# One more query product by Strassen's scheme in 128 columns, and a new order of work in a step, in a fused attention kernel

## The chip, the cores and the metric

The kernel runs on one core of a Trainium2 chip. The core has five engines with instruction queues of their own, each worked off in order: TensorE (PE: matmuls into PSUM, with weight loads beside them), VectorE (DVE), ScalarE (ACT), GpSimd (POOL) and SyncE (SP, which here issues nearly all DMAs). They meet through semaphores: an instruction waits until the ones it needs are done, and all behind it on its queue wait with it. The metric is the device time of one execution in microseconds (us), the median of several runs.

## The reference

All is float32: 64 batches of 128 tokens with 512 features, 16 heads of 64, one key and one value head for all of them.

```python
def layernorm(x, g):
    mean = jnp.mean(x, axis=-1, keepdims=True)
    var = jnp.var(x, axis=-1, keepdims=True)
    return (x - mean) * jax.lax.rsqrt(var + EPS) * g

xn = layernorm(x, g_in)
q = (xn @ Wq).reshape(b, n, H, DH).transpose(0, 2, 1, 3) * scale
kv = xn @ Wkv
k, v = (kv[..., :DH], kv[..., DH:])
# a null key and value are put ahead of k and v
sim = jnp.einsum('bhid,bjd->bhij', q, k)
sim = sim + bias
# causal mask, then the mask of the batch
attn = jax.nn.softmax(sim, axis=-1)
out = jnp.einsum('bhij,bjd->bhid', attn, v)
out = out.transpose(0, 2, 1, 3).reshape(b, n, INNER)
out = out @ Wo
result = x + layernorm(out, g_out)
```

## The kernel before

The 64 batches go in 32 steps of two. Step `d` treats batches `a = 2d` and `b = 2d + 1`: their scores and softmax. In the same step it does the attention over the values and the output projection for the pair before (`p`, `p + 1`, with `p = 2d - 2`), the output's norm and the residual for the pair before that (`l`, `l + 1`), and half of the queries of a whole group `g` of four batches that comes later. Two steps make up a group: `h = 0` (an even step) and `h = 1` (an odd one). Tokens for a still later group are loaded as `x`, normed (`two_stats`, `two_nmr`, `norm_apply`), transposed on DVE (`tokens_T`, tile `xb`), sent to DRAM and read back as `xT` (`tokens_out`, `tokens_in`).

The query product multiplies a matrix of weights with a matrix of tokens by Strassen's scheme: seven products of half size in place of eight, with sums of weights (once) and of tokens (`token_sum`, on POOL, tiles `xS1` to `xS4`) ahead, and sums of results behind. A product of half size in one step is four matmuls of 256 columns (`product_two`, L588 and on). In the steps 4 to 29, written out by `turn_full` and `body_full`, the products 2, 3 and 4 are done by the same scheme once more: seven matmuls of 128 columns (`inner_products`), with token sums of their own (`token_sums_inner`, tiles `xI`, POOL), and with sums of results, which DVE adds into the query tiles `qT` (`inner_out`). I call them inner groups 2, 3 and 4; their results stand in PSUM tiles `pi2`, `pi3`, `pi4`. Each has a slot that is used several times: the first product (sum "00"), then the sixth ("01"), then the seventh ("11" or "1*"): PE must wait for DVE's sum over one before it puts the next one in. Inner group 3 puts three of its seven products straight into the PSUM tile `pc` of product 5. Product 7 is done at full size before: `product_two(g, h, 7, ...)` into `pa`. The output projection goes by the scheme too, one level: `out_product` 1 to 7, eight records of 256 columns each, with sums `out_sum` on POOL.

Nothing is scheduled by a program: the order on every engine is the order of the calls. A step is a `turn_full` (scores of `a` and `b`, product 1, the attention over the values of the pair `p`) and a `body_full` (the rest). PSUM is full: tiles take turns in named rooms. The ones that matter below:

- `ps_q` "c": the key/value product `pkv` of `kv_pair` at the start of `body_full`, then product 5 (`pc`). `kv_pair_out` empties it: values by DVE (`vT`, L421), then keys by ACT (`kT`, L431), then a DMA copies the keys to the other partitions.
- `ps_s` "s": the output norm `yn` of batch `l` (`pair_norm`), later inner group 4.
- `ps_y` "Y" and "X" and `ps_w` "w": output products, and "Y" the norm of `l + 1` ahead of output product 5.

The statistics of the output (`rso`) and of the tokens (`rsx`) go from DVE to POOL (a power, L306) and back to DVE (`nmo`, `nmx`, L312). The softmax: maximum on DVE (`scores_max`, L812), exponentials on ACT (`exps`), reciprocal on DVE (`rinv`, L839), scaling on POOL (`scale`, L843), then the transpose of the whole probabilities on DVE (`blocks_T`, L859, tile `sb`). POOL also adds bias and mask for the scores to come (`bias_add`, L745).

SBUF: tokens `x` have four buffers, the residuals `res` two of their own; `load_res` for the pair `p` is issued in the middle of a step, for use in the next.

Of the kernel before, what the change touches and what calls it, by code (L numbers as in the profile page):

```python
# [17 lines left out]
def kernel(  # L18
# [82 lines left out]
    XB = 4  # L101
# [19 lines left out]
    rp = ctx.enter_context(tc.tile_pool(name="rp", bufs=2))  # L121

    xs, res, m8s = {}, {}, {}

    def load_x(m, queue=nc.sync):
        g, t = divmod(m, GB)
        pool, tag = (rp, "res") if m in (XB + 1, XB + 2) else (xp, "x")
        xs[m] = wM if m == XB else pool.tile([P, DIM], FP, tag=tag, name=f"x_{m}")
# [7 lines left out]
    def load_res(b):  # L136
        pool, tag = (rp, "res")
        if b >= B - 5:
            pool, tag = (gp, "xT") if b == B - 1 else (xp, "x")
        res[b] = pool.tile([P, DIM], FP, tag=tag, name=f"res_{b}")  # L140
        nc.sync.dma_start(out=res[b], in_=x[b])

    gp = ctx.enter_context(tc.tile_pool(name="gp", bufs=2))
# [272 lines left out]
    def kv_pair_out(m, pkv):  # L416
        g, t = divmod(m, GB)
        if t == 0:
            vTs[g] = hp.tile([P, GB, N], FP, tag="kv", name=f"vT_{g}", bufs=1)
        two = slice(t, t + 2)  # L420
        nc.vector.tensor_scalar(  # L421
            vTs[g][V_ROWS, two],
            pkv[V_ROWS].rearrange("p (t n) -> p t n", t=2),
            nkv[V_ROWS],
            None,
            ALU.subtract,
        )
        src = pkv[K_ROWS].rearrange("p (t i q) -> p t i q", t=2, i=NQ)
        out = kT[K_ROWS, :, two].rearrange("p i t q -> p t i q")
        for at, to, n in ((0, 0, 2), (3, 2, 1), (2, 3, 1)):  # L430
            nc.scalar.activation(  # L431
                out[:, :, to : to + n],
                src[:, :, at : at + n],
                AF.Identity,
                bias=nkv[K_ROWS],
            )
        nc.sync.dma_start(out=kT[V_ROWS, :, two], in_=kT[K_ROWS, :, two])

# [190 lines left out]
    def quarters(w):  # L629
# [4 lines left out]
    wN = const.tile([P, 3, 2, P], FP, name="wN")  # L634
    v12 = wM.rearrange("p (i h m) -> p i h m", i=2, h=2)
# [3 lines left out]
        4: (a22, v12[:, 0], v12[:, 1], wR),  # L639
    }  # L640
# [17 lines left out]
    def token_sums_inner(g, k):  # L658
# [4 lines left out]
            4: xS.get((g, 4)),  # L663
        }[k]
        b11, b12, b21, b22 = b[:, 0, 0], b[:, 1, 0], b[:, 0, 1], b[:, 1, 1]
        n = 3 if k == 4 else 4
# [12 lines left out]
    A2, A1, A0 = range(3)  # L679

    def inner_room(k, g, h):
        if k < 4:
            inner[k] = ps_w.tile([P, 4, N], FP, "w", f"pi{k}_{g}_{h}", again=(k == 3))
        else:
            two = ps_s.tile([P, 2, 4, N], FP, tag="s", name=f"pi4_{g}_{h}")
            inner[k] = two[:, 0]

    def inner_products(k, g, h, which):

        for i in which:  # L690
            if k == 3 and i in (2, 3, 4):
                n = {2: 0, 3: 1, 4: 2}[i]
                to = prod["c"].rearrange("p f (t n) -> p (f t) n", t=2)[:, n]
# [3 lines left out]
            nc.tensor.matmul(  # L697
                to,
                inner_w[k][i][:, h],
                inner_x[k, g][i],  # L700
                start=(i == 1),
                stop=True,
                skip_group_check=(i != 1),
            )

    DEST = {2: (0, 0), 3: (0, 1), 4: (1, 0)}
# [268 lines left out]
    def out_sum(p, k, eng=nc.gpsimd):  # L975
# [3 lines left out]
        if k == 0:  # L979
            yS[p] = bp.tile([P, HC, N], FP, tag="yS", name=f"yS_{p}", bufs=1)  # L980
# [120 lines left out]
    def turn(d):  # L1101
# [25 lines left out]
        values_out(p, po)  # L1127

    def turn_full(d):
# [21 lines left out]
        if d == 4:  # L1151
            token_sum(g, 1)
            token_sum(g, 2)
# [6 lines left out]
        values_out(p, po)  # L1160

# [107 lines left out]
    def body_end(d):  # L1269
# [4 lines left out]
        for r in range(p, B if last else p + 2):  # L1274
            load_res(r)
# [140 lines left out]
    def body(d):  # L1416
# [89 lines left out]
        for r in (p, p + 1):  # L1506
            load_res(r)
# [12 lines left out]
        if d == 2:  # L1520
            weight_sums_inner(4, (1, 2, 4))
        if d == 3:
# [35 lines left out]
        if d == 3:  # L1558
            weight_sums_inner(3, (3,), nc.gpsimd)
            weight_sums_inner(4, (3,))  # L1560
        out_product(p, 4, ps_y, "X", start=False)
        out_part(p + 1, 0, "X", False)

    def body_full(d):
# [6 lines left out]
        on = two_stats((ys[l], ys[l + 1]), "o")  # L1571
        if sums:
            token_sums_inner(g, 2)
            token_sum(g, 3)
        pkv = kv_pair(g * GB + 2 * h, (ps_q, "c"))
        nmrs[l], nmrs[l + 1] = two_nmr(*on, "o")
        if xw:
            xn = two_stats((xs[m], xs[m + 1]), "x")
        kv_pair_out(g * GB + 2 * h, pkv)
        if h == 1 and xw:  # L1580
            load_mask(g + 1)
        product_two(g, h, 6, ps_q, "a", start=False)
        pair_norm(l)
        scores_max(a, 1)
        keep_two("a", g, h, "u2")
        inner_room(2, g, h)
        inner_products(2, g, h, (1,))
        inner_out(2, g, h, "00")
        exps(b, 0, 3, 4)
        scores_max(b, 1)  # L1590
        if xw:
            xnmr[m], xnmr[m + 1] = two_nmr(*xn, "x")
        pair_gain(l)
        pair_residual(l)
        store(l)
# [4 lines left out]
        out_keep(p, "X", "yp1")  # L1600
        out_sum(p, 1)
        out_sum(p, 2)
        pair_norm(l + 1, (ps_y, "Y"))
        if xw:
            norm_apply(m)
        product_two(g, h, 5, ps_q, "c")
        exps(b, 0, 4)
        pair_gain(l + 1)
        inner_products(2, g, h, (6,))
        inner_out(2, g, h, "01")  # L1610
        out_product(p, 2, ps_w, "w")
        out_part(p, 0, "w")
        out_sum(p, 3)
        if xw:
            norm_apply(m + 1)
            tokens_T(m)
        pair_residual(l + 1)
        store(l + 1)
        rinv(b, 0)
        if xw:  # L1620
# [4 lines left out]
        for r in (p, p + 1):  # L1625
            load_res(r)
        if m + 2 < B and xw:
            load_x(m + 2)
            load_x(m + 3)
        exps(a, 1, 0, 4)  # L1630
        product_two(g, h, 7, ps_q, "a", start=False)
# [4 lines left out]
        if sums:  # L1636
            token_sums_inner(g, 3)
            token_sums_inner(g, 4)
        inner_room(3, g, h)
        inner_products(3, g, h, (1,))  # L1640
        q_out_two(g, h, 1, 1, "c", "u3")
        inner_out(3, g, h, "00")
        out_product(p, 5, ps_y, "Y")
        exps(a, 1, 4)
        rinv(a, 1)
        scale(a, 1)
        scale(b, 0)
        out_keep(p, "Y", "yp5")
        inner_products(3, g, h, (6, 5))
        inner_out(3, g, h, "01")  # L1650
        inner_products(2, g, h, (4, 3))
        inner_out(2, g, h, "01,10")
        inner_room(4, g, h)
        inner_products(4, g, h, (1,))
        inner_out(4, g, h, "00")
        exps(b, 1, 0, 3)
        if h == 1:
            values_T(g)
        out_product(p, 6, ps_y, "X", start=False)
        out_keep(p, "X", "yu2")  # L1660
        inner_products(3, g, h, (7,))
        exps(b, 1, 3)
# [213 lines left out]
```

## Time and profile before

| | us |
|---|---|
| median of 3 runs | 1038.99 (1038.73 to 1039.65) |
| the profiled execution | 1038.65 |
| its span, from the first instruction to the last | 1036.5 |
| ACT busy | 663.2 (64%) |
| POOL busy | 775.4 (75%) |

The granted clock of TensorE was 0.999 of full speed in this execution. A row of the timeline tells the start and the length in microseconds, the engine, the line of the program, the operation, the tile that it writes and those that it reads, the shape, how many records are merged, and in brackets how long the engine was idle just before and what released it. One float32 matmul of the program leaves two records. A matmul's length goes to the modelled end of its way through the array, so that rows of PE overlap: how fast PE works is read from one start to the next.

### The profile page before, as it was taken

What the parts mean: (1) busy time and instruction counts of PE and PEld (TensorE: products, weight loads), DVE (VectorE), ACT (ScalarE), POOL (GpSimd) and SP (SyncE); (2) the same over time, 40 slices, a digit from 0 to 9 for tenths busy, and PEclk for the clock granted to TensorE, in tenths of its full rate; (3) what the DMA queues carried; (4) which work ended last, traced back from release to release, by engine and by line L of the source; (5) the groups of instructions that cost most, each with busy time, mean ns of one, the idle gap of its engine ahead of it and who ended that gap; (6) DMA issues with size and microseconds to landing.
All of it is one profiled execution on the core that took longest, in us unless ns stands there. A gap on an engine that the chain in (4) does not pass through costs nothing.

```text
span 1036.5 us, 31871 instructions
## 1 busy us (share of the span) xinstructions
PE 1025.7 (99%) x12649; PEld 893.9 (86%) x12649; DVE 863.0 (83%) x1849; ACT 663.2 (64%) x2675; POOL 775.4 (75%) x621
## 2 busy tenths in 40 slices
PE   9999999999999999999999999999999999999997
PEld 8888888888888888888888888888888888888886
DVE  6877778888888888889888888888888888887788
ACT  5766677656577566685666766566765657756583
POOL 4997679587785877858678686786858769586786
PEclk9999999999999999999999999999999999999999
DMA  7415143151521415224152341524315152141221
GB/s 216 137 30 151 63 136 97 39 146 64 147 91 67 115 60 154 86 83 116 46 165 71 92 127 37 158 65 135 98 39 145 64 145 93 68 101 35 68 83 62
DMA packets 73836, 100.89 MB, mean 97 GB/s; under 512 B 32212, under 2 KB 36056, under 8 KB 71896
## 3 DMA queue, kind: packets, MB, share of 16 engines
q1 hardware_dynamic: 73392, 98.47, 31.8%
q8 instruction: 99, 1.62, 0.6%
q14 instruction: 49, 0.40, 0.1%
q10 hardware_dynamic: 296, 0.40, 0.1%
HBM read 63.19 MB, written 33.55 MB: 93 GB/s over the span
## 4 chain that ended last, share of the span: by engine, by line
PE 85%; DVE 10%; POOL 2%; ACT 1%; issue 1%; DMA 0%; POOLq 0%; DVEq 0%; ACTq 0%
PE pyX L1007 18%; PE pi L697 11%; PE pyY L1007 10%; PE pa L603 10%; PE pyw L1007 5%; PE pc L603 5%; PE po L920 4%; PE pkv L404 4%; PE pq L499 3%; PE sc_Y L790 3%; DVE s L805 3%; PE pa L554 2%; DVE st L301 2%; PE ps L790 2%; PE pc L697 2%; PE sc_X L790 1%
## 5 line engine op out<-in xcount | busy, mean ns | idle before, releaser
L821 ACT ACTIVATE s<-s,nmax 128x65 f32<-128x65 f32 (+1 forms) x1024 | 372.5, 372 | 75.0 <-DVE nmax L812 75.0
L843 POOL TENSOR_TENSOR s<-s,rinv 128x512 f32<-128x512 f32 (+1 forms) x132 | 189.7, 1448 | 103.7 <-DVE rinv L839 103.7
L745 POOL TENSOR_TENSOR s<-biasp,mneg 128x1552 f32<-128x1552 f32 (+1 forms) x65 | 206.1, 3172 | 45.8 <-ACT mneg L732 39.9
L821 ACT ACTIVATION_READ_ACCUMULATOR s<-s,nmax 128x1 f32 x1024 | 200.6, 196 | 0.0
L725 DVE TENSOR_TENSOR qT<-pi,qT 128x128 f32<-128x128 f32 (+1 forms) x376 | 123.7, 340 | 20.7 <-PE pi L697 15.5
L1043 ACT COPY y<-pyX 128x256 f32<-128x256 f32 x29 | 10.8, 373 | 185.6 <-PE pyX L1007 185.6
L812 DVE TENSOR_REDUCE nmax<-s 128x8 f32<-128x1032 f32 (+1 forms) x128 | 122.0, 953 | 0.9
L859 DVE STREAM_TRANSPOSE sb<-s 128x1536 f32<-128x1536 f32 (+1 forms) x68 | 112.4, 1656 | 1.7 <-POOL s L843 1.7
L1007 PE MATMUL pyX<-wT,oT 128*128 128x256 f32 x464 | 109.7, 379 | 0.0
L1007 PE MATMUL pyX<-wo,oT 128*128 128x256 f32 x464 | 109.7, 379 | 0.0
L987 POOL TENSOR_TENSOR oT<-oT 128x512 f32<-128x512 f32 x64 | 81.1, 1279 | 15.0 <-PE pyw L1007 12.8
L1007 PEld LDWEIGHTS pyX<-wT,oT 128*128 128x128 f32 x464 | 84.0, 190 | 9.2
L1007 PEld LDWEIGHTS pyX<-wo,oT 128*128 128x128 f32 x464 | 84.0, 190 | 9.2
L920 PEld LDWEIGHTS po<-sb,vr 32*64 32x64 f32 x3232 | 71.3, 130 | 13.6 <-issue 9.5
L920 PE MATMUL po<-sb,vr 32*64 32x128 f32 (+1 forms) x3232 | 82.6, 300 | 0.1
L920 PE MATMUL po_s<-sb,vr 32*64 32x128 f32 (+1 forms) x864 | 65.3, 301 | 0.0
L404 PE MATMUL pkv<-xT,wkv 128*128 128x256 f32 x256 | 63.3, 391 | 0.0
L939 ACT ACTIVATE oT<-po,nv 128x512 f32<-128x512 f32 (+1 forms) x101 | 61.6, 654 | 0.3 <-PE po L920 0.3
L1007 PE MATMUL pyY<-wo,oT 128*128 128x256 f32 x256 | 60.5, 379 | 0.0
L1007 PE MATMUL pyY<-wT,yS 128*128 128x256 f32 x256 | 60.5, 379 | 0.0
L1007 PE MATMUL pyw<-wo,oT 128*128 128x256 f32 x256 | 60.5, 379 | 0.0
L431 ACT ACTIVATE kT<-pkv,nkv 64x64 f32<-64x64 f32 (+1 forms) x96 | 24.4, 320 | 47.8 <-DVE vT L421 47.6
(231 smaller groups left out, 2637.3 us busy)
## 6 DMA issues: line engine op xcount, KB each, us to landing
res<-in_x_dram SPq DMA_DIRECT2D x64, 256.0 KB
out_dram<-y SPq DMA_DIRECT2D x63, 256.0 KB
x<-in_x_dram SPq DMA_DIRECT2D x62, 256.0 KB
xd<-xb SPq DMA_DIRECT2D x14, 1024.0 KB
xT<-xd SPq DMA_DIRECT2D x56, 256.0 KB
vr<-vd SPq DMA_DIRECT2D x64, 128.0 KB
kT<-kT SPq DMA_DIRECT2D x32, 64.0 KB
vd<-vb SPq DMA_DIRECT2D x32, 64.0 KB
```

Source lines behind the costliest of these rows:

```text
L404: nc.tensor.matmul(pkv, wkv[:, kc, :], xT[g][:, t : t + 2, kc, :], start=(kc == 0), stop=(kc == KC - 1),)
L603: nc.tensor.matmul(prod[tag][:, i], w[:, kc, f * P : (f + 1) * P], t[:, :, kc, :], start=first, stop=(kc == HK - 1), skip_group_check=not ...
L697: nc.tensor.matmul(to, inner_w[k][i][:, h], inner_x[k, g][i], start=(i == 1), stop=True, skip_group_check=(i != 1),)
L725: nc.vector.tensor_tensor(o, p, o, ALU.add)
L745: nc.gpsimd.tensor_tensor(S[b][:, :, keys], biasp[:, :, keys], mneg[:, t, keys] .unsqueeze(1) .broadcast_to([P, R8, keys.stop - keys.start ...
L812: nc.vector.tensor_reduce(nmax[b][:, hf], S[b][:, :, WITH_NULL[hf]], AX.X, ALU.max, negate=True)
L821: nc.scalar.activation(row, row, AF.Exp, bias=nmax[b][:, hf, k : k + 1], accum_out=rsum[b][:, hf, k : k + 1],)
L843: nc.gpsimd.tensor_tensor(sv, sv, rinvs[b, hf][:, lo:hi].unsqueeze(2).broadcast_to([P, hi - lo, sv.shape[2]]), ALU.mult,)
L859: nc.vector.transpose(sbs[b][:, :, lo:hi].rearrange("p j e q -> p e j q"), S[b][:, lo:hi, 1 : ROW - 1].rearrange("p e (j k) -> p e j k", k=Q),
L920: nc.tensor.matmul(po[s][rows, to : to + n], vr[g][quad, t, PLACE[j], :], sb[quad, slots, r * NF : (r + 1) * NF, :], start=(turn == 0), st ...
L987: eng.tensor_tensor(o, a, b, op)
L1007: nc.tensor.matmul(prod[key], h[:, c, :], w[:, c, :], start=(start and c == 0), stop=(c == HC - 1), skip_group_check=not start,)
```

## The change

The seventh product becomes inner group 7 in the steps 4 to 29: weights `wV` hold its sums (made in the steps 2 and 3), `token_sums_inner(g, 7)` its token sums, three of its products go straight into `pa`, and its slot takes the room "s" ahead of inner group 4. In `kv_pair_out` ACT's keys come ahead of DVE's values. In `body_full` the statistics of the tokens come ahead of those of the output, `norm_apply`, `tokens_T` and the transfers of tokens come early in the step, the score maximum of `a` comes ahead of the values, and the sums of inner groups 3 and 4 change places with the reciprocal. At the end of an odd step `next_sums` does three token sums and the sums of inner group 2 for the next group, where two token sums stood; the even step no longer does the other ones. Residuals lose their own buffers: `step_home` takes a third tile from the ring of the two `sb` tiles in each step, for the residuals of the pair `l` and for the sum `yS`, and loads them as the step begins; the last eight residuals go into the weights of the queries, which are idle by then. The tokens `x` have two buffers in place of four.

```diff
-    XB = 4
+    XB = 2
+    def step_home(d):
+
+        t = hp.tile([P, 6, R8, Q], FP, tag="sb", name=f"home_{d}")
+        parts = t.rearrange("p (i j) e q -> p i (j e q)", i=3)
+        yS[2 * d - 2] = parts[:, 2].rearrange("p (c n) -> p c n", n=N)
+        if d > 1:
+            for i in range(2):
+                load_res(2 * d - 4 + i, parts[:, i])
+
+    def late_res(b):
+
+        i = b - (B - 8)
+        load_res(b, wq[:, i // 2, (i % 2) * DIM : (i % 2 + 1) * DIM])
...
     # kv_pair_out
-        nc.vector.tensor_scalar(vTs[g][V_ROWS, two], ...)
         for at, to, n in ((0, 0, 2), (3, 2, 1), (2, 3, 1)):
...
         nc.sync.dma_start(out=kT[V_ROWS, :, two], in_=kT[K_ROWS, :, two])
+        nc.vector.tensor_scalar(vTs[g][V_ROWS, two], ...)
...
     ROOMS = {
+        7: (s3, wV[:, 0], wV[:, 1], wV[:, 2]),
+    NATIVE = {3: "c", 7: "a"}
-    DEST = {2: (0, 0), 3: (0, 1), 4: (1, 0)}
+    DEST = {2: (0, 0), 3: (0, 1), 4: (1, 0), 7: (1, 0)}
...
+    def next_sums(g):
+
+        for k in (1, 2, 3):
+            token_sum(g, k)
+        token_sums_inner(g, 2)
...
     # body_full
         if sums:
-            token_sums_inner(g, 2)
-            token_sum(g, 3)
+            token_sums_inner(g, 7)
+        if xw:
+            xn = two_stats((xs[m], xs[m + 1]), "x")
+        on = two_stats((ys[l], ys[l + 1]), "o")
         pkv = kv_pair(g * GB + 2 * h, (ps_q, "c"))
+            xnmr[m], xnmr[m + 1] = two_nmr(*xn, "x")
         nmrs[l], nmrs[l + 1] = two_nmr(*on, "o")
+        scores_max(a, 1)
         kv_pair_out(g * GB + 2 * h, pkv)
+            norm_apply(m)
+            norm_apply(m + 1)
         product_two(g, h, 6, ps_q, "a", start=False)
...
-        product_two(g, h, 7, ps_q, "a", start=False)
+        inner_room(7, g, h)
+        inner_products(7, g, h, (2, 3, 4))
         keep_two("a", g, h, "u3")
...
+        inner_products(7, g, h, (6,))
+        inner_out(7, g, h, "01")
         out_keep(p, "Y", "yp5")
         inner_products(3, g, h, (6, 5))
         inner_out(3, g, h, "01")
+        inner_products(7, g, h, (7, 5))
+        inner_out(7, g, h, "1*")
+        inner_out(7, g, h, "*1")
+        rinv(a, 1)
+        scale(a, 1)
...
         inner_products(3, g, h, (7,))
+        inner_out(3, g, h, "1*")
+        inner_out(3, g, h, "*1")
+        inner_products(3, g, h, (2, 3, 4))
         rinv(b, 1)
         blocks_T(a)
         scale(b, 1)
         bias_add(b + 2)
-        if h and xw:
-            token_sum(g + 1, 1)
-            token_sum(g + 1, 2)
+        if h == 1 and xw:
+            next_sums(g + 1)
         inner_products(4, g, h, (6,))
         inner_out(4, g, h, "01")
-        inner_out(3, g, h, "1*")
-        inner_out(3, g, h, "*1")
-        inner_products(3, g, h, (2, 3, 4))
```

DVE in an odd step (step 13), from the transpose of the values to the transpose of the probabilities of `a` and the sums behind it; before:

```order
L442 STREAM_TRANSPOSE vb_7_5832<-vT_7_5316 64x512
L1034 COPY y_24_5739<-pyX_24_1_5734 128x256
L839 RECIPROCAL rinv_27_1_5853<-rsum_27_5669 128x8
L859 STREAM_TRANSPOSE sb_26_5855<-s_26_5256 128x8x6x32
L725 TENSOR_TENSOR qT_7_1_0_5575<-pi4_7_1_5826,qT_7_1_0_5575 128x2x64
L725 TENSOR_TENSOR qT_7_1_1_5576<-pi3_7_1_5801,qT_7_1_1_5576 128x4x64
L725 TENSOR_TENSOR qT_7_1_1_5576<-pi3_7_1_5801,qT_7_1_1_5576 128x2x2x64
```

And the same place of the changed kernel:

```order
L457 STREAM_TRANSPOSE vb_7_5917<-vT_7_5390 64x512
L1055 COPY y_24_5827<-pyX_24_1_5802 128x256
L744 TENSOR_TENSOR qT_7_1_0_5648<-pi4_7_1_5928,qT_7_1_0_5648 128x2x64
L744 TENSOR_TENSOR qT_7_1_1_5649<-pi3_7_1_5872,qT_7_1_1_5649 128x4x64
L744 TENSOR_TENSOR qT_7_1_1_5649<-pi3_7_1_5872,qT_7_1_1_5649 128x2x2x64
L858 RECIPROCAL rinv_27_1_5937<-rsum_27_5742 128x8
L878 STREAM_TRANSPOSE sb_26_5939<-s_26_5324 128x8x6x32
L744 TENSOR_TENSOR qT_7_1_0_5648<-pi4_7_1_5928,qT_7_1_0_5648 128x2x64
```

The first sum of inner group 4 and the two wide sums of inner group 3 have moved between the copy and the reciprocal; the sum over group 4's sixth product still comes right behind the transpose.

POOL from the end of step 11 (bias for batch 25) into step 12 (the scaling of batch 24); before:

```order
L745 TENSOR_TENSOR s_25_5064<-biasp_89,mneg_121 128x1552
L546 TENSOR_TENSOR xS1_7_5066<-xT_7_4980 128x512
L546 TENSOR_TENSOR xS2_7_5068<-xT_7_4980,xS1_7_5066 128x512
L745 TENSOR_TENSOR s_26_5256<-biasp_89,mneg_121 128x1552
L843 TENSOR_TENSOR s_24_4858<-s_24_4858,rinv_24_0_5270 128x8x64
L306 TENSOR_TENSOR rso_5283<-rso_5283,nhalf_113 128x2
L677 TENSOR_TENSOR xI2_7_5292<-xT_7_4980 128x256
L677 TENSOR_TENSOR xI2_7_5292<-xT_7_4980,xI2_7_5292 128x128 x2
L546 TENSOR_TENSOR xS3_7_5296<-xT_7_4980 128x512
L306 TENSOR_TENSOR rsx_5307<-rsx_5307,nhalf_113 128x2
```

And the same place of the changed kernel:

```order
L764 TENSOR_TENSOR s_25_5131<-biasp_86,mneg_118 128x1552
L561 TENSOR_TENSOR xS1_7_5133<-xT_7_5002 128x512
L561 TENSOR_TENSOR xS2_7_5135<-xT_7_5002,xS1_7_5133 128x512
L561 TENSOR_TENSOR xS3_7_5137<-xT_7_5002 128x512
L695 TENSOR_TENSOR xI2_7_5139<-xT_7_5002 128x256
L695 TENSOR_TENSOR xI2_7_5139<-xT_7_5002,xI2_7_5139 128x128 x2
L764 TENSOR_TENSOR s_26_5324<-biasp_86,mneg_118 128x1552
L862 TENSOR_TENSOR s_24_4914<-s_24_4914,rinv_24_0_5338 128x8x64
L695 TENSOR_TENSOR xI7_7_5353<-xS3_7_5137 128x128
L695 TENSOR_TENSOR xS3_7_5137<-xS3_7_5137 128x128
L695 TENSOR_TENSOR xI7_7_5353<-xS3_7_5137,xI7_7_5353 128x128 x2
L321 TENSOR_TENSOR rsx_5359<-rsx_5359,nhalf_110 128x2
```

The third token sum and the sums of inner group 2 have moved from the even step's start ahead of the bias for batch 26 in the odd step; in the even step the sums of inner group 7 stand between the scaling and the first power.

More of the change, by code (lines that the diff above doesn't have):

```diff
@@ L437, in kv_pair_out @@
         nc.sync.dma_start(out=kT[V_ROWS, :, two], in_=kT[K_ROWS, :, two])
+        nc.vector.tensor_scalar(
+            vTs[g][V_ROWS, two],
+            pkv[V_ROWS].rearrange("p (t n) -> p t n", t=2),
+            nkv[V_ROWS],
+            None,
+            ALU.subtract,
+        )
     def values_T(g):
@@ L1273, in body_end @@
         lo, hi = (0, R8 // 2), (R8 // 2, R8)
[L1274 to L1275 removed]
+        for r in range(p, B) if last else range(l, p + 2):
+            late_res(r)
         scores_max(a, 1)
```

146 lines of the change are left out of this document (69 added, 77 removed).

## The prediction

> **What bounds the kernel now.** I read the page first, then the busy time by stage over two steps, then the timeline of each engine inside these two steps. TensorE (PE) is busy all the time:
>
> ```profile
> span 1036.5 us, 31871 instructions
> PE 1025.7 (99%) x12649; PEld 893.9 (86%) x12649; DVE 863.0 (83%) x1849; ACT 663.2 (64%) x2675; POOL 775.4 (75%) x621
> ```
>
> The 26 full steps (4 to 29) alternate. Below are step 12 (even) and step 13 (odd), each from its key/value product to the next one; columns after the time are PE, PEld, DVE, ACT, POOL:
>
> ```profile
> 415.73:447.79 32.06, 31.85 (x399) 27.39 (x395) 27.18 (x59) 20.87 (x85) 26.04 (x25) 1.00 0.21 69
> 447.79:479.08 31.29, 31.29 (x399) 27.52 (x395) 26.92 (x60) 19.96 (x83) 21.24 (x15) 1.00 0.47 128
> ```
>
> Both hold the same 399 matmul records, yet the even step is 0.77 longer, though PE looks busy: a matmul's end is modelled, so waits hide in busy time, and I go by start-to-start times. The odd step, PE:
>
> ```profile
> 456.98 1.89 PE L603 MATMUL pa<-xS,wq 128*128 128x256 f32 x8
> 458.70 0.38 PE L697 MATMUL pi<-xI,wq 128*128 128x128 f32 x2
> 458.92 0.39 PE L697 MATMUL pi<-xI,wL 128*128 128x128 f32 x2
> ...
> 461.32 0.61 PE L697 MATMUL pi<-xI,wN 128*128 128x128 f32 x4
> ...
> 462.44 1.89 PE L1007 MATMUL pyX<-wT,oT 128*128 128x256 f32 x8
> 464.17 0.38 PE L697 MATMUL pi<-xI,wS 128*128 128x128 f32 x2
> ...
> 465.28 1.89 PE L1007 MATMUL pyX<-wo,oT 128*128 128x256 f32 x8
> 467.10 0.49 PE L697 MATMUL pi<-xS,wq 128*128 128x128 f32 x2
> ```
>
> Four matmuls of 256 columns (8 records) take 1.73 (456.98 to 458.70), one of 128 takes 0.22. After the product at 465.28 PE was ready at 467.01 and began at 467.10: 0.09 lost. The even step:
>
> ```profile
> 419.51 1.89 PE L1007 MATMUL pyX<-wo,oT 128*128 128x256 f32 x8
> 421.58 1.99 PE L603 MATMUL pc<-xS,wS 128*128 128x256 f32 x8 [0.18 <-ACT kT L431]
> ...
> 433.88 1.89 PE L1007 MATMUL pyX<-wo,oT 128*128 128x256 f32 x8
> 435.81 0.49 PE L697 MATMUL pi<-xS,wq 128*128 128x128 f32 x2
> 436.13 0.39 PE L697 MATMUL pi<-xI,wM 128*128 128x128 f32 x2
> ```
>
> Query product 5 (`pc`) was ready at 421.24 and began at 421.58: 0.34. At 435.81 the wait is 0.20, and the next start follows after 0.32 in place of 0.22: a wait costs 0.10 more, until the next matmul has caught up. So the odd step holds 0.19 of stall and the even one 0.45 + 0.30 + a remainder of 0.21 (0.77 + 0.19 - 0.75). Without stalls both would take 31.10. This is the measure for the change: what it takes off PE's columns, and what VectorE (DVE) and GpSimd (POOL) then let PE wait.
>
> **Columns.** Four matmuls of 256 columns (1.73) become seven of 128 (7 x 0.222 = 1.55): -0.18 a step. This is certain to come off PE, whatever comes after.
> The Trainium skill, page "TensorE: Matmul & The Clock Gate", section "Back-to-back issue gap", speaks against it: in a stream of loads and matmuls it gives some 81 ns at 128 columns and 131 at 512, so about 98 at 256 on a straight line, an estimate; seven against four would then cost 1.45 times as much, +0.8 a step. The rows above (0.22 against 0.43) do not bear this out here, and it has no part in the sum.
>
> **The late transpose, every step.** PE cannot start the last three products of inner group 4 (`pi4`, at 467.10) until DVE has added their predecessor, which stands behind the transpose of the probabilities. DVE, odd step:
>
> ```profile
> 460.24 0.68 DVE L621 TENSOR_TENSOR qT<-pc,qT 128x512 f32<-128x512 f32 x1
> ...
> 461.97 0.29 DVE L725 TENSOR_TENSOR qT<-pi,qT 128x128 f32<-128x128 f32 x1 [0.38 <-PE pi L697]
> ...
> 463.07 0.71 DVE L442 STREAM_TRANSPOSE vb<-vT 64x512 f32<-64x512 f32 x1
> 464.37 0.42 DVE L1034 COPY y<-pyX 128x256 f32<-128x256 f32 x1 [0.59 <-PE pyX L1007]
> 465.02 0.20 DVE L839 RECIPROCAL rinv<-rsum 128x8 f32<-128x8 f32 x1 [0.23 <-ACT s L821]
> 465.14 1.73 DVE L859 STREAM_TRANSPOSE sb<-s 128x1536 f32<-128x1536 f32 x1
> 466.79 1.04 DVE L725 TENSOR_TENSOR qT<-pi,qT 128x128 f32<-128x128 f32 x3
> ```
>
> Now the copy comes 0.20 after the output product ends (464.17), and only reciprocal and transpose stand between it and the sum at 466.79; 466.79 + 0.29 + 0.02 is PE's 467.10. After the change three sums go ahead of the reciprocal: the first of group 4 (0.21) and the two wide ones of group 3 (with the wait of the second for the first 0.45 + 0.33; the row of three shows 0.96 for all). From the output product's end: 0.20 + copy 0.33 + 0.21 + 0.78 + reciprocal 0.12 + transpose 1.65 + 0.31 = 3.60. PE meanwhile has five 128-column matmuls, the first of group 4 that now comes later, and one output product: 6 x 0.222 + 1.73 = 3.06. It waits 0.54 + 0.10 = 0.64, and nothing earlier can mend that, since the copy itself waits for PE. Even: 0.64 for 0.30, **+0.34**. In the odd step the transpose of the values (0.71) lies between: from PE's last product of group 7 DVE has two wide sums (0.78), reciprocal 0.12, query sum 0.60, wide sum 0.33, that transpose 0.63, about 2.5, where PE's two small products and the output product leave 2.2; the copy is 0.3 late. Odd: 0.94 for 0.19, **+0.75**. Bounds: 0.4 to 0.9 of wait, by whether the sums follow each other without the dependence's wait.
>
> **The wait inside group 7, every step.** Its last two products need DVE's sum over its sixth. The row at 461.97 starts 0.04 after its matmuls' end (461.93); one matmul lasts 0.38, the sum 0.29: 0.38 + 0.04 + 0.29 + 0.02 = 0.73, while PE fills 3 x 0.22 = 0.66 with products 6 and 5 of group 3. **+0.07, +0.10: 0.17.** Bounds 0 to 0.2.
>
> **The key/value room, even steps.** Product 5 takes the bank that the key/value product leaves, and waits for keys (ACT) and values (DVE). The keys now need no DVE. The values stand behind the tokens' and the output's statistics and the score maximum, and the statistics behind POOL:
>
> ```profile
> 465.30 1.91 POOL L843 TENSOR_TENSOR s<-s,rinv 128x1024 f32<-128x1024 f32 x1 [0.72 <-DVE rinv L839]
> 467.17 3.20 POOL L745 TENSOR_TENSOR s<-biasp,mneg 128x1552 f32<-128x1552 f32 x1
> 471.13 1.28 POOL L546 TENSOR_TENSOR xS<-xT 128x512 f32<-128x512 f32 x1 [0.76 <-DMA xT<-xd]
> 472.49 1.28 POOL L546 TENSOR_TENSOR xS<-xT,xS 128x512 f32<-128x512 f32 x1
> 473.71 3.24 POOL L745 TENSOR_TENSOR s<-biasp,mneg 128x1552 f32<-128x1552 f32 x1
> ...
> 478.26 1.05 POOL L843 TENSOR_TENSOR s<-s,rinv 128x512 f32<-128x512 f32 x1 [1.31 <-DVE rinv L839]
> ```
>
> At an odd step's end POOL now works 11.65 from the scaling (465.30) to 476.95, 0.76 of it waiting for tokens that will come earlier, and then idles 1.31. The change adds the third token sum and inner group 2's sums:
>
> ```profile
> 417.15 0.73 POOL L677 TENSOR_TENSOR xI<-xT 128x256 f32<-128x256 f32 x1
> ...
> 418.92 1.27 POOL L546 TENSOR_TENSOR xS<-xT 128x512 f32<-128x512 f32 x1
> 420.29 0.69 POOL L306 TENSOR_TENSOR rsx<-rsx,nhalf 128x2 f32<-128x2 f32 x1
> ...
> 429.01 0.46 POOL L677 TENSOR_TENSOR xI<-xS 128x128 f32<-128x128 f32 x1
> ...
> 430.92 1.91 POOL L843 TENSOR_TENSOR s<-s,rinv 128x1024 f32<-128x1024 f32 x1
> ```
>
> That is 1.77 (417.15 to 418.92) + 1.24 = 3.0, in all 13.9 from the scaling. The scaling starts 0.16 after the late transpose does, and from that transpose to the next step's start it is 479.08 - 465.14 = 13.94. So POOL is done 0.1 after the step's start T, not 2.1 before it. Then: scaling 1.05, group 7's sums 1.91 (as group 4's, 429.01 to 430.92), the two powers 0.65 + 0.72, so 4.45; DVE's two factors 0.25, maximum 1.2, values 0.5:
>
> ```profile
> 449.28 0.33 DVE L312 TENSOR_SCALAR nmo<-mvo,rso 128x1 f32<-128x1 f32 x2 [0.81 <-POOL rso L306]
> ...
> 451.26 0.49 DVE L421 TENSOR_SCALAR vT<-pkv,nkv 64x256 f32<-64x256 f32 x1
> 451.78 1.23 DVE L812 TENSOR_REDUCE nmax<-s 128x8 f32<-128x1032 f32 x1
> ```
>
> The bank is free at T + 6.43; PE is ready at T + 5.51 (419.51 + 1.73 - 415.73). It waits 0.92 + 0.10 for 0.45: **+0.57**. In odd steps POOL has no such work ahead; the values end near T + 5.1, and nothing waits. Bounds: 0.3 to 1.0.
>
> **The rest.** The remainder of 0.21 in even steps goes: the sums of group 3 move up. In its place DVE, late by its values, frees the bank of the second output norm about 0.2 after product 5 of the output wants it: 0.3, net **+0.09**. DVE's four added sums (about 1.1) lie in its 4.4 idle a step, except where counted. Stores queue behind the tokens' transfers on SP, and have a whole step before their buffers are wanted; residuals are loaded as a step begins and wanted some 8 later; late residuals and new homes add no instruction to PE. I take all these at 0; if the SP queue's cover failed, up to 0.5 a step. Weight sums of group 7 (four, DVE, steps 2 and 3): 0, at most 1.7. Step 4 takes its token sums right ahead of the first scaling: between 0 and the 3.0 that they add; I take 1.3, beside what every even step gets.
>
> **Sum.** Even: -0.18 + 0.34 + 0.17 + 0.57 + 0.09 = +0.99; odd: -0.18 + 0.75 + 0.17 = +0.74. Thirteen odd steps +9.6, eleven even ones +10.9, step 4 +2.3, step 28 (no tokens left to norm, so the values are nearly in time) +0.6: +23.4. The profiled execution took 1038.65 us (span 1036.5), the median of three is 1038.99, so they stand as equal: **1062 us**.
>
> **Rivals.**
> - Half of it: the transposes and the key/value room hold at their lower bounds, group 7's wait and the late values vanish: odd -0.18 + 0.25 = +0.1, even -0.18 + 0.2 + 0.4 - 0.2 = +0.2 to +0.6, some +5 to +11 in all: 1044 to 1050. For it: these terms are differences of 0.1 to 0.3. Against: the 3.60 against 3.06 is a sum of rows.
> - Faster: POOL ends its longer chain before it is wanted (it decides if the bias sum of the odd step ends before T - 0.9), so that keys first and norm first clear all early waits: even -0.18 - 0.45 - 0.21 + 0.34 = -0.5, odd +0.27 without the late values; 13 x -0.23 = -3: 1036. If the transpose is not late either, 26 x (31.10 - 0.18) against 13 x 63.35 is -20: 1019. For it: POOL idles 1.31 there now. Against: it gets 3.0 more.
> - No difference: the -0.18 and lost stalls balance the late transposes: 1037 to 1041.
>
> **How the numbers follow.** Forecast 0.62, half of it 0.20, faster 0.11, no difference 0.07. Range 1044 to 1068, up to +29 by the upper bounds; it leaves out the faster and equal cases. About 0.2% (2 us) is what a measurement can tell here: faster 0.11, same 0.07, slower 0.82.
>
> **What would show it.** After: odd steps near 32.0 and even ones near 33.0 between key/value products. The late transpose starting about 1.6 after its output product's end, PE's first wait behind it 0.5 or more in each step. POOL's last bias sum of an odd step ending at the next step's start, and `pc` at T + 6.4 in even steps, T + 5.5 in odd ones. Seven 128-column products of group 7 at 0.22 each. It would be wrong if the transpose's wait is under 0.2, or the even `pc` comes before T + 5.8.

## The result, and the profile after

The changed kernel takes 1195.77 us (median of four runs, 1193.02 to 1201.10) where the kernel before takes 1039.32 on the same chip: a ratio of 1.151, interval 1.146 to 1.156. Slower was forecast; +156 us in place of +23, far outside the range, was not. The page of the profiled execution (1193.02 us), where before had PE at 99% and the granted clock at 9 in every slice:

```profile
span 1191.2 us, 32455 instructions
PE 1058.4 (89%) x12805; PEld 921.0 (77%) x12805; DVE 885.2 (74%) x1957; ACT 663.3 (56%) x2675; POOL 796.6 (67%) x673
...
PE   9999999699896996969969799698897997989997
...
PEclk9999999899897998989989999899898998999999
...
L1057 ACT COPY y<-pyY 128x256 f32<-128x256 f32 x32 | 11.9, 371 | 154.4 <-DMA out_dram<-y 141.5
```

PE has gaps now, at regular distances, and the clock falls with them. The last row (a group of section 5 of the page: busy time and mean, then the idle time ahead of it and who ended it) names an instruction that waited for no DMA before: ACT's copy of an output product into the output tile `y` waits 141.5 us for stores, 6.0 to 11.45 us in each of twelve odd steps and some 2 in even ones. By stage, steps 12 and 13 (columns as in the prediction; the last three are the granted clock, the busy share of the DMA engines and GB/s):

```profile
471.21:503.81 32.60, 31.77 (x406) 27.60 (x401) 27.39 (x63) 20.97 (x85) 24.88 (x25) 1.00 0.16 53
503.81:546.77 42.96, 33.21 (x405) 29.00 (x400) 28.08 (x64) 19.94 (x83) 24.02 (x19) 0.88 0.39 105
```

The even step is 32.60, where 33.05 was forecast and 32.06 stood before; the odd one is 42.96, where 32.03 was forecast and 31.29 stood before. The twelve odd steps from 5 to 27 make up 139 of the 155 us by which the span is longer. The chain in step 13 (start T = 503.81) follows, from the timelines of SP, ACT, DVE and PE. A row SPq is the issue of DMAs by SP, and its length is that of the issuing: `xd<-xb` is `tokens_out`, `xT<-xd` is `tokens_in`, `x<-in_x_dram` is `load_x`, and `out_dram<-y` is the two stores.

```profile
510.25 0.33 SPq L391 DMA_DIRECT2D xd<-xb  x1
514.22 1.75 SPq L399 DMA_DIRECT2D xT<-xd  x4
516.08 1.21 SPq L138 DMA_DIRECT2D x<-in_x_dram  x2
517.38 0.95 SPq L1101 DMA_DIRECT2D out_dram<-y  x2
...
527.84 0.37 ACT L1057 COPY y<-pyY 128x256 f32<-128x256 f32 x1 [11.08 <-DMA out_dram<-y]
...
531.34 0.20 DVE L858 RECIPROCAL rinv<-rsum 128x8 f32<-128x8 f32 x1 [8.89 <-ACT s L840]
531.46 1.73 DVE L878 STREAM_TRANSPOSE sb<-s 128x1536 f32<-128x1536 f32 x1
533.11 0.25 DVE L744 TENSOR_TENSOR qT<-pi,qT 128x128 f32<-128x128 f32 x1
...
533.42 0.80 PE L716 MATMUL pi<-xS,wq 128*128 128x128 f32 x2 [9.49 <-DVE qT L744]
534.01 0.64 PE L716 MATMUL pi<-xI,wM 128*128 128x128 f32 x2
534.44 0.63 PE L716 MATMUL pi<-xS,wq 128*128 128x128 f32 x2
```

SP, DVE's first residual and ACT's copy in the same step before (T = 447.79), and last the first residual after (`y<-yn,home`):

```profile
455.35 0.69 DVE L1077 TENSOR_TENSOR y<-yn,res 128x512 f32<-128x512 f32 x1
...
456.07 3.10 SPq L1080 DMA_DIRECT2D out_dram<-y  x2
459.50 0.33 SPq L376 DMA_DIRECT2D xd<-xb  x1
463.43 1.76 SPq L384 DMA_DIRECT2D xT<-xd  x4
...
461.52 0.37 ACT L1036 COPY y<-pyY 128x256 f32<-128x256 f32 x1 [0.17 <-PE pyY L1007]
...
512.32 0.69 DVE L1098 TENSOR_TENSOR y<-yn,home 128x512 f32<-128x512 f32 x1
```

Before, the first store went out as soon as its residual was done, at T + 8.3. After, `tokens_out`, `tokens_in` and `load_x` stand ahead of it on SP; SP stands still from 510.58 to 514.22 until the tokens have reached DRAM, and issues the store at T + 13.6, though its first residual was done at 513.01. Its landing then takes until 527.84, another 10.5. Tiles `y` have three buffers, and `y` of batch `p + 1` = `l + 3` takes the buffer of `y` of batch `l`, the one that is being stored in the same step. ACT wants to write it at 516.76 and waits 11.08. Behind that copy stand `b`'s last exponentials, behind these `rinv(b, 1)`, then the transpose of `a`'s probabilities, then DVE's sum (533.11) that PE's `pi4` wants: PE idles 9.49 us. When it starts, its next products of 128 columns come 0.43 apart (534.01, 534.44) in place of 0.22; by windows the clock is 0.52 for 3 us and then full:

```profile
533.40:536.40 3.00, 2.98 (x10) 2.71 (x11) 1.55 (x4) 0.00 (x0) 3.00 (x2) 0.52 0.00 0
536.40:546.70 10.30, 10.30 (x281) 8.85 (x279) 8.48 (x16) 4.21 (x23) 9.54 (x9) 1.00 0.01 3
```

That is about 1.4 us more in such a step, an estimate (3.00 x 0.48): of the 11.67 that step 13 is longer than before, 9.49 is the idle time and 1.4 the clock. The Trainium skill, page "TensorE: Matmul & The Clock Gate", section "Part 1: The HAM clock gate", says that the array falls to half its clock after an idle window of some 3.4 us and needs as long a busy one to recover; the trace agrees (9.49 idle, then 3.0 at 0.52).

### The profile page after: what moved, and what is told of

Its sections match the earlier page's. It is cut to its first block, busy times and chain, and to the rows that moved or that the text cites. A ratio compares the mean times of both kernels' runs of the same rounds, so it can differ in the third digit from the quotient of the medians.

```text
span 1191.2 us, 32455 instructions
## 1 busy us (share of the span) xinstructions
PE 1058.4 (89%) x12805; PEld 921.0 (77%) x12805; DVE 885.2 (74%) x1957; ACT 663.3 (56%) x2675; POOL 796.6 (67%) x673
## 4 chain that ended last, share of the span: by engine, by line
PE 65%; DMA 13%; DVE 9%; ACT 7%; POOL 3%; issue 2%; SPq 0%; POOLq 0%; ACTq 0%; DVEq 0%
DMA out_dram<-y 12%; PE pyX L1028 9%; PE pyY L1028 9%; PE pa L618 7%; PE pi L716 7%; ACT s L840 6%; PE po L939 5%; PE pkv L419 5%; DVE sb L878 4%; PE pyw L1028 4%; PE pc L618 4%; PE pq L514 2%; PE ps L809 2%; PE sc_Y L809 2%; PE sc_X L809 2%
## 5 line engine op out<-in xcount | busy, mean ns | idle before, releaser
L744 DVE TENSOR_TENSOR qT<-pi,qT 128x128 f32<-128x128 f32 (+1 forms) x480 | 157.4, 342 | 80.9 <-PE pi L716 75.5
L716 PE MATMUL pi<-xS,wq 128*128 128x128 f32 x260 | 61.6, 322 | 116.7 <-DVE qT L744 116.7
L716 PEld LDWEIGHTS pi<-xS,wq 128*128 128x128 f32 x260 | 46.1, 212 | 131.8 <-DVE qT L744 127.1
L858 DVE RECIPROCAL rinv<-rsum 128x8 f32<-128x8 f32 (+1 forms) x132 | 25.7, 194 | 106.3 <-ACT s L840 106.0
L1057 ACT COPY y<-pyY 128x256 f32<-128x256 f32 x32 | 11.9, 371 | 154.4 <-DMA out_dram<-y 141.5
L939 PEld LDWEIGHTS po<-sb,vr 32*64 32x64 f32 x3232 | 71.4, 130 | 13.6 <-issue 9.5
L1028 PE MATMUL pyY<-wo,oT 128*128 128x256 f32 x256 | 76.4, 453 | 0.0
L1028 PEld LDWEIGHTS pyY<-wo,oT 128*128 128x128 f32 x256 | 58.2, 237 | 9.3
```

The costliest lines, as they stand in the source:

```text
L716: nc.tensor.matmul(to, inner_w[k][i][:, h], inner_x[k, g][i], start=(i == 1), stop=True, skip_group_check=(i != 1),)
L744: nc.vector.tensor_tensor(o, p, o, ALU.add)
L939: nc.tensor.matmul(po[s][rows, to : to + n], vr[g][quad, t, PLACE[j], :], sb[quad, slots, r * NF : (r + 1) * NF, :], start=(turn == 0), st ...
L1028: nc.tensor.matmul(prod[key], h[:, c, :], w[:, c, :], start=(start and c == 0), stop=(c == HC - 1), skip_group_check=not start,)
```

## The experiments

Theory A: the stores' place on SP, the copy waiting for their landing, and what stands behind it on ACT. Theory B: the odd steps are slow by the seventh product or the new order themselves, and the store only shows it. Theory C: the clock fell by the load. Each kernel was timed beside the kernel before on its chip.

**e1_stores_first**: the changed kernel, with the stores first again.

```diff
     tokens_T(m + 1)
-            if h == 1:
-                tokens_out(g + 1)
-                tokens_in(g + 1)
-            if m + 2 < B:
-                load_x(m + 2)
-                load_x(m + 3)
...
         store(l + 1)
+        if xw:
+            if h == 1:
+                tokens_out(g + 1)
+                tokens_in(g + 1)
+            if m + 2 < B:
+                load_x(m + 2)
+                load_x(m + 3)
```

> The changed kernel with tokens_out, tokens_in and the two load_x put behind the second store of a step; the transposes of the tokens stay where the change put them. Theory A (the stores stand on SP behind the tokens' transfers, the copy y<-pyY of the second sequence waits for the store's landing on ACT, and the exponentials, rinv and TensorE wait behind it): the wait of 11 us goes from the odd steps, which come to about 32.0 to 32.5 us, the even ones to 32.6 to 33.2, and the time to about 1060 to 1068 us. Theory B (the seventh product or the new order of the transposes makes the odd steps slow by itself, and the store's landing only shows it): the odd steps stay above 42 us and the time above 1180. Theory C (the clock fell from 0.999 to 0.95 by the load of the seven products, not by the idle time): the granted clock stays near 0.95 and the time near 1110. If the keys' room on POOL is late once the odd steps no longer wait, even steps have the kv products' start at about 6.4 us after the step's start; if not, at 5.5.

1073.94 us, 1.033 times before (1.032 to 1.035), clock 1.000; 122 us are gone by this one move. B and C fall: the seven products and the order on all engines but SP are unchanged. The two steps:

```profile
428.25:461.41 33.16, 31.92 (x405) 27.62 (x401) 27.98 (x63) 21.07 (x85) 25.67 (x26) 1.00 0.16 52
461.41:494.01 32.60, 31.84 (x405) 27.85 (x400) 27.98 (x64) 19.88 (x82) 22.91 (x18) 1.00 0.47 138
```

The total is 6 us above the expected band, and the odd steps are 0.1 above theirs; this comes back below.

**e2_four_y**: four buffers for `y`, all orders kept.

```diff
-  tag="y", name=f"y_{b}", bufs=3
+  tag="y", name=f"y_{b}", bufs=4
```

> The changed kernel with four buffers for y instead of three, all orders kept: the stores stay behind the tokens' transfers on SP. Theory A in its full form (what costs is that y of the second sequence takes the buffer of a y of the same step, whose store is late): the copy no longer waits, odd steps come to 32.0 to 32.5 us, the time to 1058 to 1068 us. Theory A2 (the SP queue itself is what is late, by its loads of x too): the store's wait goes and the next transfer's takes its place, odd steps 36 to 42 us, the time 1110 to 1170. Theory B: unchanged, above 1180.

1072.45 us, 1.032 (1.031 to 1.034), 4 us above the expected band and no slower than e1. The store is as late as before (its odd step starts at 461.55), and nobody waits:

```profile
475.05 0.90 SPq L1101 DMA_DIRECT2D out_dram<-y  x2
...
474.63 0.37 ACT L1057 COPY y<-pyY 128x256 f32<-128x256 f32 x1
```

So a late store costs nothing by itself: it is the buffer that it holds.

**e3_before_late**: the kernel before, with only its two `store` calls moved behind `load_x(m + 3)`.

```diff
-        store(l)
...
-        store(l + 1)
...
                 load_x(m + 3)
+        store(l)
+        store(l + 1)
```

> The kernel before (eight products) with its two stores of a step put on SP behind tokens_out, tokens_in and the loads of x, nothing else changed. Theory A: the odd steps get the wait, some 8 to 14 us each over 13 odd steps, and the time comes to 1140 to 1220 us, with the copy y<-pyY waiting on the stores. Theory B (the seventh product or the transposes are needed for it): no change, 1037 to 1042 us.

1376.12 us, 1.325 (1.323 to 1.327): the loss needs nothing of the seventh product. It is more than I expected: in this kernel the loads of residuals and of `x` stand later, and they now hold the stores in even steps too (in step 8 the store goes out 13.3 us after the step's start, and the copy waits 7.23). Step 9 and step 10 take 50.93 and 41.43. The waits of ACT:

```profile
ACT y L1036 <- DMA out_dram<-y: 283.3, 25, 18.3
```

**e7_loads_last** and **e8_stores_before_in**: the changed kernel, where on SP the stores come ahead of `load_x` alone (e7), or ahead of `tokens_in` and `load_x` (e8).

```diff
-            if m + 2 < B:
-                load_x(m + 2)
-                load_x(m + 3)
...
         store(l + 1)
+        if xw:
+            if m + 2 < B:
+                load_x(m + 2)
+                load_x(m + 3)
```

That is e7; in e8 `tokens_in(g + 1)` of odd steps moves along, ahead of the loads.

> The changed kernel with only the two loads of x put behind the stores; tokens_out and tokens_in stay ahead of them. Theory A1 (tokens_in): the stores go 1.2 us earlier only, the wait of the odd steps stays at 8 to 10 us, 1165 to 1190. Theory A4 (the loads of x are what holds the stores): as e1_stores_first, 1071 to 1078.

> The changed kernel with tokens_out left where the change put it, and the two stores put between tokens_out and tokens_in; the loads of x stay behind tokens_in. Theory A1 (what delays the stores is that SP stands still at tokens_in until the tokens are back in memory, and the stores and their landing come behind that): as e1_stores_first, 1071 to 1078 us. Theory A3 (what delays them is that their bytes share the DMA engines with the 1 MB of tokens_out): the wait on the stores stays in the odd steps, 1120 to 1195.

e8 gives 1072.52 (1.032, 1.030 to 1.034), e7 1135.15 (1.091, 1.086 to 1.095). In e8 the store goes out at 470.90 and the copy finds its buffer free at 474.75; in e7 it goes out at 491.75, behind `tokens_in`, and lands at 498.13:

```profile
468.11 0.33 SPq L391 DMA_DIRECT2D xd<-xb  x1
470.90 2.06 SPq L1101 DMA_DIRECT2D out_dram<-y  x2
...
474.75 0.37 ACT L1057 COPY y<-pyY 128x256 f32<-128x256 f32 x1
```

```profile
489.89 1.76 SPq L399 DMA_DIRECT2D xT<-xd  x4
491.75 0.85 SPq L1101 DMA_DIRECT2D out_dram<-y  x2
...
498.13 0.37 ACT L1057 COPY y<-pyY 128x256 f32<-128x256 f32 x1 [5.61 <-DMA out_dram<-y]
```

For e7 my expectation was wrong: it counted only the 1.2 us in which SP issues the loads. From issue to landing a store takes at most 3.9 us behind `tokens_out` (e8), 6.4 behind the 1 MB of `tokens_in` (e7), 10.5 behind that and the 0.5 MB of `x` (after). What is issued ahead costs its transfer, too. Step 27 of the changed kernel, where no `x` is left to load, agrees: it takes 38.19, as the odd steps of e7 do (35.78 to 39.33). The Trainium skill, page "DMA: Bandwidth & Descriptors", section "Queues, rings and completion order", says that all DMAs issued by SP use one row of rings, which each DMA engine consumes in order. These three numbers agree with it; no run here tells waiting in the ring from sharing the DMA engines.

The next runs ask for the terms of the prediction, and then for a kernel that keeps the change and beats both. Each builds on the one before unless said otherwise.

**e4_late_pi4** (on e1): inner group 3's two wide sums behind group 4's sum "01" on DVE.

```diff
         inner_products(3, g, h, (7,))
-        inner_out(3, g, h, "1*")
-        inner_out(3, g, h, "*1")
...
         inner_out(4, g, h, "01")
+        inner_out(3, g, h, "1*")
+        inner_out(3, g, h, "*1")
```

> The stores first as in e1_stores_first, and the scheme's group-3 copies 1* and *1 put on DVE behind group 4's copy 01, so that the sum for the seventh product of group 4 is taken earlier. Theory (late transpose): the wait of the first product of pi4 behind the DVE sum goes, 0.3 to 0.7 us less a step than e1_stores_first, 8 to 18 us in all (about 1047 to 1056). Rival (DVE's next work, the sums of the second token matrix, becomes late by as much): the same within 2 us as e1_stores_first.

1061.99 us, 11.95 less than e1 in the same comparison: odd steps 31.85 for 32.60. Even steps gain less, 32.88 for 33.17 in the median: their wait behind the transpose goes as well, but after the shorter odd step POOL's bias sum ends later, at T + 0.18 for T + 0.04, and product 5 waits longer (0.97 for 0.83 in step 12).

**e5_powers_early** (on e4): group 7's token sums behind the powers on POOL.

```diff
-        if sums:
-            token_sums_inner(g, 7)
...
         nmrs[l], nmrs[l + 1] = two_nmr(*on, "o")
+        if sums:
+            token_sums_inner(g, 7)
```

> e4_late_pi4 with the four sums for group 7 put on POOL behind the two powers of the norms (even steps only). Theory (the values, and with them product 5, are late because POOL's powers stand behind these sums): the start of product 5 moves from T + 6.5 to T + 5.5 or so in even steps, the wait before pyY<-wT,home goes too, even steps from 32.8 to 31.6, the time to 1044 to 1050 us. Rival (the sums for group 7 are late in turn, TensorE waits for them before the products 2, 3, 4 of group 7): 1055 to 1063.

1046.53 us, 1.0075 (1.006 to 1.009). Product 5 starts at 425.08 in a step that starts at 419.54, T + 5.54, and even steps come to 31.4 to 32.4.

**b1_all, b2_all, b6_rinv_first** (on e5): the values are emptied ahead of the maximum, the values' transpose goes into DVE's idle time behind the first sum of group 3, and products 7 and 5 of group 7 go behind products 4 and 3 of group 2. In b1 their two sums go there as well, but the query sum of `pc` and `u3` stays where it was, so it reads group 7's result without them: the queries of b1 are incomplete, and its time speaks for the order alone. b2 moves reciprocal, scalings and query sum along, in this order behind group 7's sums; b6 puts reciprocal and scalings ahead again. The middle of b6 against the changed kernel:

```diff
         inner_out(3, g, h, "01")
-        inner_products(7, g, h, (7, 5))
-        inner_out(7, g, h, "1*")
-        inner_out(7, g, h, "*1")
         rinv(a, 1)
         scale(a, 1)
...
-        q_out_two(g, h, 1, 1, "c", "u3")
         inner_products(2, g, h, (4, 3))
         inner_out(2, g, h, "01,10")
+        inner_products(7, g, h, (7, 5))
+        inner_out(7, g, h, "1*")
+        inner_out(7, g, h, "*1")
+        q_out_two(g, h, 1, 1, "c", "u3")
```

> e5_powers_early, and: the values' scaling ahead of the score maximum on DVE, the transpose of the values of odd steps into DVE's idle time behind the sums of group 3, and products 7 and 5 of group 7 with their two sums behind products 4 and 3 of group 2. If these are the waits that are left: odd steps 31.0 to 31.3, even ones 31.0 to 31.6, the time 1024 to 1036 us, faster than before. If something else comes late: 1038 to 1050.

> As b1_all, but the sums of group 7 stay ahead of the query sum that reads them: products 7 and 5 of group 7, their sums, the reciprocal, the scaling and the query sum all behind products 4 and 3 of group 2. If the waits before product 5, before pyY<-wT,home, inside group 7 and behind the values' transpose are what is left of the loss: odd steps 31.0 to 31.3, even ones 31.1 to 31.9, the time 1030 to 1037 us, faster than before by 0.2 to 0.8%. If the query sum is late in turn for the products 2, 3, 4 of group 3: 1038 to 1050.

> b2_all with the second reciprocal and the two scalings on POOL put back ahead of product group 2's last sum, so that the transpose of the probabilities no longer waits 0.55 us for POOL. Theory (that wait is what was late in b2_all: 0.4 us and 0.1 more in every step): odd steps 31.1 to 31.2, even ones 31.2 to 32.1, 1031 to 1038 us. Rival (the query sum, not the transpose, holds TensorE): 1044 to 1049.

b1 1035.22, b2 1047.12, b6 1035.13 (ratio 0.9965, 0.995 to 0.998). b2 missed: its odd steps are 31.64, since POOL scales later and the transpose of the probabilities waits for it (DVE of b2, then an odd step by windows, step 11 of b2 and of b6):

```profile
407.38 1.78 DVE L878 STREAM_TRANSPOSE sb<-s 128x1536 f32<-128x1536 f32 x1 [0.55 <-POOL s L862]
...
389.73:421.37 31.64, 31.38 (x405) 27.68 (x400) 28.02 (x64) 19.95 (x83) 23.00 (x18) 1.00 0.47 139
...
384.99:416.09 31.10, 31.10 (x404) 27.75 (x401) 28.05 (x64) 19.95 (x83) 22.72 (x18) 1.00 0.47 137
```

**b4_maxima_late** (on b2) and **b5_all_late** (on b6): on DVE the first sum of group 2 goes ahead of the tokens' transposes, the first maximum behind them, and the second behind the residual of `l + 1` (b4) or behind the first sum of group 3 (b5).

> b2_all, and on DVE the first sum of group 2 ahead of the tokens' transposes, the first score maximum behind them, the second behind the second residual and store. Theory (in even steps of b2_all DVE's late start of the step is paid by TensorE at pi<-xI,wL and at pyY<-wT,home): both waits go, even steps 31.0 to 31.3, 1024 to 1031 us. Rival (the later maxima make the exponentials, and with them rinv and the transpose of the probabilities, late): 1032 to 1050.

> b6_rinv_first, with DVE's start of a step as in b4_maxima_late (first sum of group 2 ahead of the tokens' transposes, the first maximum behind them, residuals early), and the second maximum put into DVE's idle time behind the first sum of group 3. If each wait that is left in b2_all and b4_maxima_late has been named rightly: odd and even steps 30.9 to 31.2, 1020 to 1029 us. If DVE only hands the lateness on: 1030 to 1040.

b4 1048.51: its even steps became regular at 32.0, but the gain that I expected lay behind b2's POOL wait, and DVE's sum for the output part, now behind the second maximum, was late for PE by up to 0.4. b5 1031.25 (0.992, 0.991 to 0.994), in the band of DVE handing on some of the lateness, yet faster than before. Its steps:

```profile
415.52:446.61 31.09, 31.09 (x405) 27.60 (x401) 27.78 (x63) 20.92 (x85) 25.58 (x25) 1.00 0.17 55
446.61:477.95 31.34, 31.20 (x405) 27.76 (x401) 27.96 (x64) 19.85 (x82) 23.06 (x18) 1.00 0.52 144
```

**b7_sum_on_pool** (on b5): step 3 takes 34.99 in e1 and in b5, 33.15 before. In e1 the extra time stands behind DVE's last two weight sums (DVE, POOL and PE of e1):

```profile
130.22:165.21 34.99, 34.01 (x396) 29.25 (x391) 28.88 (x59) 22.23 (x92) 27.09 (x23) 1.00 0.43 124
...
155.97 3.73 DVE L673 TENSOR_TENSOR wq<-wq 128x256 f32<-128x256 f32 x2
...
156.13 3.30 POOL L764 TENSOR_TENSOR s<-biasp,mneg 128x1552 f32<-128x1552 f32 x1 [0.72 <-DVE sb L878]
...
162.82 0.43 PE L939 MATMUL po_s<-sb,vr 32*64 32x256 f32 x2 [0.98 <-DVE s L826]
```

```diff
-            weight_sums_inner(7, (3,))
+            weight_sums_inner(7, (3,), nc.gpsimd)
```

> b5_all_late, with the last weight sum for group 7 in step 3 given to POOL. Theory (step 3 is longer by 1.6 us behind its score products since DVE's second weight sum runs beside POOL's bias sum and takes 3.43 us, where such a sum takes 0.42 elsewhere): step 3 from 34.99 to 33.3 to 33.5 us, 1029 to 1030.5 us for the whole. Rival (the step is longer for another reason of the seventh product): step 3 stays at 34.9 to 35.0, 1031 to 1032 us.

Step 3 comes to 33.42, as expected; 1030.14 us in all, 0.991 of before (0.989 to 0.993). That whole differs from b5's by no more than the intervals; the step is what shows it. On DVE one weight sum is left there, at 156.60, and it takes 0.42:

```profile
130.85:164.27 33.42, 33.42 (x395) 29.04 (x391) 26.02 (x58) 22.59 (x94) 26.36 (x21) 1.00 0.44 127
```

## Why the prediction was wrong, and where it was right

**The step that failed** is the one on the stores: "Stores queue behind the tokens' transfers on SP, and have a whole step before their buffers are wanted". The first half was read rightly from the order; the second was not worked out. Three buffers mean that `y` of `l + 3` wants the buffer of `y` of `l`, and in the trace of before that copy runs in the same step, 5.45 us after the store is issued (456.07 and 461.52). The cover was 5.45 less the landing, not a step. In its place the copy waited 11.08 us and PE 9.49 in step 13, and an odd step grew by 11.67. The price set on a failure was wrong as well: "if the SP queue's cover failed, up to 0.5 a step" had no row behind it. The trace of before had what was needed: the 3.9 us that SP takes from `tokens_out` to `tokens_in`, and ACT's copy with exponentials, reciprocal, scaling and transpose queued behind it. e1, e2 and e8 take away 122 to 123 of the 156 us in three ways, and e3 makes such a loss in the kernel before.

With that cover restored (e1) the other terms can be weighed one by one. PE of e1, even step (T = 428.25), then odd:

```profile
432.03 1.89 PE L1028 MATMUL pyX<-wo,oT 128*128 128x256 f32 x8
...
434.59 2.00 PE L618 MATMUL pc<-xS,wS 128*128 128x256 f32 x8 [0.67 <-DVE vT L446]
...
447.17 1.89 PE L1028 MATMUL pyX<-wo,oT 128*128 128x256 f32 x8
449.43 0.49 PE L716 MATMUL pi<-xS,wq 128*128 128x128 f32 x2 [0.37 <-DVE qT L744]
449.75 0.39 PE L716 MATMUL pi<-xI,wM 128*128 128x128 f32 x2
...
478.66 0.39 PE L716 MATMUL pc<-xI,wS 128*128 128x128 f32 x2
479.31 0.49 PE L716 MATMUL pi<-xI,wM 128*128 128x128 f32 x2 [0.26 <-DVE qT L744]
479.64 1.89 PE L1028 MATMUL pyX<-wo,oT 128*128 128x256 f32 x8
482.03 0.49 PE L716 MATMUL pi<-xS,wq 128*128 128x128 f32 x2 [0.50 <-DVE qT L744]
```

- **Columns: as forecast.** Products 2, 3 and 4 of group 7 in the changed kernel come 0.22 apart:

```profile
480.73 0.39 PE L716 MATMUL pa<-xS,wV 128*128 128x128 f32 x2
480.95 0.39 PE L716 MATMUL pa<-xI,wq 128*128 128x128 f32 x2
```

The steps of b5, 31.09 and 31.34, hold waits of 0.06 and 0.31 (starts at 434.63 and 460.73) with 0.10 each behind them; without these both take 30.93, and the forecast was 31.10 - 0.18 = 30.92. The rule of the Trainium skill that was weighed against this term is not borne out.
- **The late transpose: right in mechanism.** Even: ready at 448.90, began 449.43, 0.53 and 0.10 more (forecast 0.54 and 0.10). Odd: 0.66 + 0.10 (481.37 to 482.03), and 0.43 + 0.10 at 479.31, where PE waits for the first sum of group 4, which stands behind the values' transpose and the copy. Together 1.29 where 0.94 was forecast: the same lateness is paid in two places, and each pays its 0.10. Taking the two wide sums away (e4) gave back 0.75 an odd step.
- **The wait inside group 7:** forecast 0.17. In e1 PE loses 0.10 there and 0.10 on the next start, in both kinds of steps.
- **The key/value room: right, where the odd steps do not stall.** In e1 product 5 starts at 434.59, T + 6.34 (forecast T + 6.43), 0.83 after PE was ready (forecast 0.92). POOL's bias sum ends there at T + 0.04, as forecast (T + 0.1):

```profile
425.07 3.22 POOL L764 TENSOR_TENSOR s<-biasp,mneg 128x1552 f32<-128x1552 f32 x1
```

  In the changed kernel itself product 5 starts at 476.73, T + 5.52: the stalled odd step gave POOL the time to finish its bias sum before T. By the mark that I had set ("the even `pc` comes before T + 5.8") this term would have counted as wrong there; e1 shows that it was there, hidden by the larger loss, and e5, which takes it away, is 15.5 us faster than e4.
- **The rest of even steps:** the wait ahead of output product 5, forecast 0.3, is 0.37 in e1.
- **Weight sums: "0, at most 1.7":** the upper end, 1.57 by b7.

The sum gave +23.4; e1 has a span 35.5 above before's. Of the 12.1 between them 6.3 is the odd steps 5 to 27 (15.2 measured, 12 x 0.74 forecast), 2.6 the even steps 6 to 26 (13.5 measured, 11 x 0.99 forecast) and 1.8 step 3; smaller terms of both signs make up the rest. Slower was right, and the reasons given for it explain most of the 35 us that e1 still loses; the other 122 us came from the step that failed.

The rival "faster" named its 1019 us if no wait were left. With the waits taken out one after the other the kernel comes to 1030, so the change can pay, by 0.9%, in another order than it was made in.

## What to carry to other kernels

When a transfer is moved ahead of others on an issuing queue, list for each one behind it the buffer that it holds and the first instruction that wants that buffer, and read both times from the trace; the ring's size says whether that is this step or the next. Count the transfers ahead with their bytes and with the waits of the issuing engine, not with the time of the issues. And a term of the sum that looks refuted in a stalled kernel may only be covered by the stall: weigh it again when the stall is gone.

## What the runs showed of the hardware

- 9.5 us of idle PE cost some 1.4 us more, at half clock for 3 us. In e3, with two such gaps in two steps, the clock's mean fell to 0.89.
- One DVE sum of two SBUF tiles of 128 x 256 took 3.43 us beside a POOL sum of 3.30, and 0.42 elsewhere (least, median and greatest ns in e1):

```profile
L673 DVE TENSOR_TENSOR wq<-wq x3: 381/418/3432, 82.0 to 156.3; 128x256 f32<-128x256 f32 x3
```

It ended 0.3 us after POOL's. The Trainium skill, page "SBUF — State Buffer", section "SBUF: two separate sides", says that such an operation of VectorE and one of GpSimd that reads SBUF hold a pair of ports in turn, each for its whole length; the trace agrees, and b7, which takes the sum from DVE, takes away 1.57 of the 1.84 us by which step 3 was longer.
- A short wait of PE ahead of a product of 128 columns cost 0.10 us beyond its length, on the next start (0.32 or 0.33 for 0.22): in e1 at 449.43 and 482.03, in b5 at 434.63 and 460.73, after waits of 0.06 to 0.66.
